# A decoder layer on one core: sums of squared encodings and router logits with the small matrix as the stationary operand, four token chunks on four column groups of TensorE

## The chip, the core and the metric

The kernel runs on one core of a Trainium2 chip. The core has a matrix engine (TensorE, PE in the profile), a vector engine (VectorE, DVE), a scalar engine for functions such as exp (ScalarE, ACT), a general engine (GpSimd, POOL), and a queue that issues most of the transfers (SyncE, SP). TensorE reads its operands from the on-chip memory SBUF and writes to the accumulator memory PSUM. A matrix product on it has two parts: a weight load puts the *stationary* operand into the array (PEld in the profile), and the matmul itself streams the *moving* operand through it. The engines run side by side and wait for each other through semaphores.

The metric is the time of one execution on the device in microseconds (us), median of nine runs: 1785.03 us for the kernel before, the lowest 1782.12, the highest 1790.69.

## What is computed

A decoder layer over 16 sequences of 256 tokens with 256 features (4096 tokens): a first attention, a cross attention, and a mixture of four experts, each followed by a residual sum and a layer norm. The two parts that matter here are the scores of the first attention and the router of the experts. The rest is cut.

```python
# first attention, 16 heads, 8 complex components a head
qp, kp = prep(Q), prep(K)                 # tanh of one product, then a second product
qc = qp[..., :nq] + 1j * qp[..., nq:]     # kc from kp in the same way
q1 = einsum('bshn,nm->bshm', qc, Hc)      # k1 in the same way
qe = real(einsum('hcb,bshn->cshn', R, q1))   # ke in the same way
qq = sum(qe ** 2, -1)                     # one number for each token and head
kk = sum(ke ** 2, -1)
s = qq[:, :, None, :] * kk[:, None, :, :]
attn = softmax(s / s, axis=2)
out = einsum('bijh,bjhd->bihd', attn, V).reshape(B, S, D) @ wo + bo

# router of the four experts, two of which each token takes
logits = einsum('bsh,he->bse', x, router_w) + router_b + load_balancer
rw, sel = top_k(logits, 2)
rw = softmax(rw)
```

`s / s` is the ratio of a product with itself. The kernel forms it from `p * (1 / p)` for each of the two factors: a *ratio* for the query side and one for the key side.

## The kernel before

All data is float32. The tokens are handled in eight *pairs* of sequences: a pair q has 512 tokens, which are four *chunks* n of 128 tokens (`CPB = 4`, `P = 128`). In the records of the profile each float32 product is two passes of TensorE (two LDWEIGHTS and two MATMUL records); a transposition is one.

**The order is written out by hand.** PE, ACT and DVE run their instructions in the order in which the program makes them (`ORDERED`, line 27). The first attention walks through 128 steps, 16 for each pair, numbered t. A step issues on TensorE first the product of the hidden layer (`hidden`, tile `ph`, four products), then the jobs that a planner hands out, then the second product of the step before (`outer`, tile `pe`, four products). ScalarE applies tanh to `ph` twice in each step (tile `h`). The two PSUM tiles `ph` are both used in each step, so that the next step's `ph` waits until ScalarE has read them.

**The planner** (`Plan`, line 30) holds jobs with a first step, a due step and a cost in us, which is a constant of the program. Each step grants a credit (`RATE`, line 850: 2.5 up to step 64, then 2.25); `spend` takes jobs in the order of their due steps while the credit lasts, and a job that is due is taken in any case. So costs and rate decide in which step a job's instructions stand, on all three ordered engines. The cross attention has a second planner (`planB`): its steps are called quarters (`quarter`, line 1360), four to a unit of a sequence and four heads; two quarters at a time get a credit (line 1586: 2.45). In the steps before and after a middle stretch (`SINGLE = 228`) jobs are taken one at a time instead.

**What the change touches in the first attention.** After eight steps of one side (keys are side 0, queries side 1) the tile `sq` holds squared encodings, 128 partitions by 512 tokens. For pairs 0 to 3 there is one such tile with eight partitions a head, for pairs 4 to 7 there are two (`sqs`). `norms` (line 966) sums the squares of each head: for each chunk n, the chunk of `sq` (128 by 128) is the stationary operand and a matrix of ones and zeros (`b16`, or `selc` where there are two tiles; 128 by 16) is the moving one. The result has tokens on partitions: 128 by 4 by 16. VectorE takes the reciprocal (`rc`) and multiplies (`ra`). On the query side the job `queries` (line 981) then turns the four chunks of `ra` by four transpositions into rows of heads (16 by 512, tile `ptr`), VectorE copies them to SBUF (`rqT`), and SP writes them to a buffer in DRAM (`rqd`). From there `spread` (line 1001) reads rows back, each repeated over all 128 partitions (`rqb`), four steps before `scores` (line 1009) multiplies them on VectorE with the key ratios of `ra` (tile `z`); `exps` takes the exponential on ScalarE and `weigh` (line 1033) multiplies with the values on TensorE (tile `po`, eight products with a 32-column stationary operand, four heads on four column groups).

**What it touches in the cross attention.** When the residual and norm of a pair are done, `turn_tokens` (line 1497) transposes its tokens to features on partitions (`xTr`, or `x` for the last two pairs), and the job `logits` (line 1511) multiplies: for each chunk n and each half c of the features the chunk (128 by 128) is stationary, the router's weights (128 by 4) move. VectorE adds the bias from PSUM (tile `lg`), and `routing` (line 380) goes on with small steps on VectorE, GpSimd and ScalarE, one in each of the next five steps. Six steps after `logits` the job `places` (line 1524) sums up positions on TensorE, and `listing` (line 431) scatters the tokens to the experts' lists in DRAM by indirect transfers on POOL's queue. After the last pair of a group (pair 6 for the first group, pair 7 for the second) the lengths of the lists are known, and the experts begin: `begin` (line 650) loads the first rows of a list (`xe`) and transposes them on TensorE.

Three stages follow each other: the first attention to about 560 us (its end overlaps the beginning of the next), the cross attention to about 1245 us, then the experts.

Of the kernel before, what the change touches and what calls it, by code (L numbers as in the profile page):

```python
# [22 lines left out]
CPB = TB // P  # L23
# [80 lines left out]
def decoder_kernel(ctx: ExitStack, tc: tile.TileContext, a: dict, out: bass.AP):  # L104
    nc = tc.nc
    PE, DVE, ACT, POOL, SP = nc.tensor, nc.vector, nc.scalar, nc.gpsimd, nc.sync
# [8 lines left out]
    ident = const.tile([P, P], F32, tag="ident", name="ident")  # L115
# [35 lines left out]
    def mm(out_, lhsT, rhs, start=True, stop=True):  # L151
        PE.matmul(out=out_, lhsT=lhsT, rhs=rhs, start=start, stop=stop)  # L152
# [189 lines left out]
    moe, puts = {}, ([], [])  # L342
# [7 lines left out]
    def moe_setup(wb, xw, xb, tri):  # L350
        moe["pool"] = wb

        def tl(name, shape, dt=F32):
            moe[name] = wb.tile(shape, dt, tag=name, name=name)
            return moe[name]

        moe["rw"], moe["rb"], moe["tri"] = xw[:, :, D:], xb[:, D:], tri
        before = tl("before", [P, P])
        POOL.memset(before, 1.0)
        POOL.affine_select(before, before, [[1, P]], ALU.is_gt, 0.0, base=0, channel_multiplier=-1)  # L360
        POOL.memset(tl("ones", [P, P]), 1.0)
        base = tl("base", [P, 2, 4])
        for g in range(2):
            for e in range(4):
                POOL.memset(base[:, g, e:e + 1], float(e * SIZES[g]))
        tl("place", [P, NCH, 2], I32)
        tl("weight", [P, NCH, 2])
        tl("count", [P, 2, 5], I32)
        tl("length", [P, 5])
# [463 lines left out]
    tl = tails.enter_context(tc.tile_pool(name="tl", bufs=1))  # L833
    dr = tails.enter_context(tc.tile_pool(name="drA", bufs=2, space=bass.MemoryType.DRAM))
# [9 lines left out]
    def first_attention():  # L844

        plan = Plan(
            turn_x=.55, project=1.85, values=1.85, norms=1.5, rotate=1.9, queries=.5, weigh=.9, finish1=.55, finish2=.55,
            finish3=1.9, fold=.8,
        )
        RATE = (2.5, 2.25)  # L850
        wk = mat(hd, "L0_attn_wk", D)
        w1p = hd.tile([P, 2, D], F32, tag="w1p", name="w1p")
        w2T = wH.tile([16, D], F32, tag="w2T", name="w2T")
# [24 lines left out]
        xTs, qTs, sums16, ratios, rqTs, rqbs, zs, ovs, os_, ots, encs, pes = ({} for _ in range(12))  # L878

        def bank(name):  # L880
            return banks[0].tile([P, 512], F32, tag="sm", name=name)
# [84 lines left out]
        def norms(q, side, sqs):  # L966


            p16 = bank("p16")[:, :CPB * H].rearrange("p (n h) -> p n h", h=H)
            for n in range(CPB):  # L970
                for i, sq in enumerate(sqs):
                    s = b16 if len(sqs) == 1 else selc[:, i, :]
                    mm(p16[:, n, :], sq[:, n * P:(n + 1) * P], s, i == 0, i == len(sqs) - 1)
            rc = tl.tile([P, CPB, H], F32, tag="rc", name=f"rc{q}{side}", bufs=2)
            DVE.reciprocal(rc, p16)
            ra = ratios[q, side] = tl.tile([P, CPB, H], F32, tag=f"ra{side}", name=f"ra{q}{side}", bufs=2)
            DVE.tensor_tensor(ra, p16, rc, ALU.mult)
            if side == 1:
                plan.job(plan.now + 1, plan.now + 1, queries, q)

        def queries(q):

            pw = bank("ptr")
            for n in range(CPB):
                PE.transpose(pw[:H, n * P:(n + 1) * P], ratios[q, 1][:, n, :], ident)
            rqT = tl.tile([H, 512], F32, tag="rqT", name="rqT", bufs=1)
            DVE.tensor_copy(rqT, pw[:H, :])
            rqTs[q] = dr.tile([H, 512], F32, tag="rqd", name="rqd")
            SP.dma_start(out=rqTs[q], in_=rqT)
            per = 1 if q < NPAIR - 1 else 2  # L990
            t0 = 16 * q + 25 if per == 1 else plan.now + 5
            for u in range(8):
                t = t0 + 2 * u // per
                plan.at(max(t - 4, plan.now + 1), spread, q, u)
                for gp in range(2):
                    plan.at(t + gp // per, scores, q, u, gp)
                    plan.at(t + gp // per + 1, exps, q, u, gp)
                tw = t + 1 // per + 2
                plan.job(tw, tw + 2, weigh, q, u)
# [9 lines left out]
        def scores(q, u, gp):  # L1009

            b, k = divmod(u, 4)
            z = zs[u, gp] = cm.tile([P, 2, 2, S], F32, tag="z", name="z", bufs=6)
            if q == NPAIR - 1 and gp == 1:
                return
            h0 = 4 * k + 2 * gp
            rk = ratios[q, 0][:, 2 * b:2 * b + 2, h0:h0 + 2].rearrange("p j h -> p h j")
            DVE.tensor_tensor(z, bc(rqbs[u][:, 2 * gp:2 * gp + 2], 2, 2), bc(rk, 3, S), ALU.mult)  # L1017

        def exps(q, u, gp):

            b, k = divmod(u, 4)
            z = zs[u, gp]
            if q < NPAIR - 1 or gp == 0:
                ACT.activation(z, z, AF.Exp)  # L1024
                return
            for g in range(2):
                for jc in range(2):
                    h = 4 * k + 2 + g
                    ACT.activation(
                        z[:, g, jc], rqbs[u][:, 2 + g], AF.Exp, scale=ratios[q, 0][:, 2 * b + jc, h:h + 1]  # L1030
                    )

        def weigh(q, u):
# [59 lines left out]
            DVE.tensor_scalar(w1p[:, par, :], w1p[:, 1, :], mpar[:, par:par + 1], None, ALU.mult)  # L1093
        project(0, 0, 0)

        b16 = tl.tile([P, H], F32, tag="b16", name="b16")
        POOL.memset(b16, 1.0)
        POOL.affine_select(b16, b16, [[-8, H]], ALU.is_ge, 0.0, base=0, channel_multiplier=1)
        POOL.affine_select(b16, b16, [[8, H]], ALU.is_ge, 0.0, base=7, channel_multiplier=-1)
        rep = wH.tile([H, 2, 8, 16], F32, tag="rep", name="rep")  # L1100
        POOL.memset(rep, 0.0)
        for cc in range(2):
# [8 lines left out]
            )  # L1111

        b8 = wH.tile([P, 8], F32, tag="b8", name="b8")
        selc = tl.tile([P, 2, H], F32, tag="selc", name="selc")
        POOL.memset(selc, 0.0)

        def halves():

            DVE.tensor_copy(b8, b16.rearrange("p (h t) -> p h t", t=2)[:, :, 0])
            for cc in range(2):  # L1120
                DVE.tensor_copy(selc[:, cc, 8 * cc:8 * cc + 8], b8)


        b2c = hd.tile([P, 1], F32, tag="b2c", name="b2c")
# [56 lines left out]
        for q in range(NPAIR):  # L1181
# [99 lines left out]
    def cross_attention(wb, r1, ps1):  # L1281
# [7 lines left out]
        for mp in mpads:  # L1289
# [4 lines left out]

        plan = Plan(
            finish1=.55, turn_x=.55, turn_keys=.55, turn_tokens=.55, finish4=.55, project=1.05, values=1.9, finish5=1.9,
            logits=1.9, places=.6, weigh=1.85,
        )
        turned_keys = set()
        SINGLE = 32 * NPAIR - 28  # L1300
# [1 line left out]
        def apart():  # L1302
            return 1 if plan.now >= SINGLE else 2
# [5 lines left out]
        def bank(name):  # L1309
            return banks[0].tile([P, 512], F32, tag="sm", name=name)  # L1310
# [183 lines left out]
        def slack(q):  # L1494
            return 3 if roomy(q) else 0
# [13 lines left out]
                plan.job(plan.now + apart(), plan.now + apart() + slack(q), logits, q)  # L1509

        def logits(q):
            pl = bank("pl")[:, :4 * CPB].rearrange("p (n e) -> p n e", e=4)
            for n in range(CPB):
                for c in range(2):
                    mm(pl[:, n, :], xTs[q, c][:, n * P:(n + 1) * P], moe["rw"][:, c, :], c == 0, c == 1)
            lg = tiny.tile([P, CPB, 4], F32, tag="lg", name="lg")
            DVE.tensor_tensor(lg, pl, bc(moe["rb"], 1, CPB), ALU.add)
            route = routing(q, lg)
            for k in range(5):
                plan.later(1 + k, next, route, None)  # L1520
            wait = (FREE - 9 - plan.now) % 16 if roomy(q) else 0
            plan.job(plan.now + 6 + wait, plan.now + 6 + wait + slack(q), places, q)
# [49 lines left out]
        def step(t):  # L1572

            if not 0 <= t < SINGLE:
                if 0 <= t // 4 < len(units) + LAG:
                    quarter(t // 4, t % 4)
                plan.run(t)
                if t < -3 or t % 4 > 0:
                    plan.take()
                else:  # L1580
                    plan.take(6)
            elif t % 2 == 0:
                for u in (t, t + 1):
                    plan.now = u
                    quarter(u // 4, u % 4)
                plan.grant(2.45)
                plan.run(t)
                plan.run(t + 1)
                plan.spend(most={"finish1": 2, "values": 1}, like={"logits": "values"})

        return plan, step

# [107 lines left out]
```

## Time and profile before

| | us |
|---|---|
| median of nine runs | 1785.03 |
| the profiled execution | 1783.59 |
| its span, first to last instruction | 1781.9 |
| TensorE matmul busy in the span | 1642.7 |
| ScalarE busy | 970.0 |
| VectorE busy | 919.7 |
| GpSimd busy | 539.0 |
| reciprocal in `norms` (L975), 16 of 0.557 | 8.9 |
| multiplication in `norms` (L977), 16 of 0.225 | 3.6 |
| copy in `queries` (L987), 8 of 0.678 | 5.4 |
| bias in `logits` (L1517), 8 of 0.172 | 1.4 |

How to read it: an instruction is given as line, engine, operation and tile (`out<-in`). Nearly all products have line 152, a helper, so they are told apart by tile and shape. `128*16` or `128*128` behind a PE operation are the rows and columns of the stationary operand that it uses, `32*128` is one with 32 rows (one of four row groups), `128*32` one with 32 columns (one of four column groups). A matmul's duration includes the way through the array, which overlaps with the next one; what a group of matmuls really takes is the distance from its start to the start of the next group, called its *pitch* below. The granted clock of TensorE is 1.00 in most of the span, 0.5 in single windows of 3.4 us, and the mean is 0.963.

### The profile page before, as it was taken

What the parts mean: (1) busy time and instruction counts of PE and PEld (TensorE: products, weight loads), DVE (VectorE), ACT (ScalarE), POOL (GpSimd) and SP (SyncE); (2) the same over time, 40 slices, a digit from 0 to 9 for tenths busy, and PEclk for the clock granted to TensorE, in tenths of its full rate; (3) what the DMA queues carried; (4) which work ended last, traced back from release to release, by engine and by line L of the source; (5) the groups of instructions that cost most, each with busy time, mean ns of one, the idle gap of its engine ahead of it and who ended that gap; (6) DMA issues with size and microseconds to landing.
All of it is one profiled execution on the core that took longest, in us unless ns stands there. A gap on an engine that the chain in (4) does not pass through costs nothing. (4 is left out here: it accounts for less than half of the span.)

```text
span 1781.9 us, 32316 instructions
## 1 busy us (share of the span) xinstructions
PE 1642.7 (92%) x12254; PEld 963.1 (54%) x12254; DVE 919.7 (52%) x1911; ACT 970.0 (54%) x1463; POOL 539.0 (30%) x1235
## 2 busy tenths in 40 slices
PE   7999999999999899999999999979999999899761
PEld 2344444444445556666666666644675758565551
DVE  2235565556556787777777777752223424122133
ACT  4457577778787766666666666534333122223127
POOL 5000332113213232334363553645330010131421
PEclk9999999999999999999999999987999999999976
DMA  9922111122122200000000000000352101221213
GB/s 254 295 90 71 58 62 61 60 70 87 60 72 73 96 15 14 2 3 26 26 21 20 26 9 20 32 31 32 99 183 73 48 1 49 85 80 46 66 49 124
DMA packets 117771, 115.34 MB, mean 65 GB/s; under 512 B 7776, under 2 KB 111408, under 8 KB 117584
## 3 DMA queue, kind: packets, MB, share of 16 engines
q1 hardware_dynamic: 108560, 93.08, 16.4%
q0 software_dynamic: 7824, 19.65, 3.7%
q8 instruction: 114, 1.87, 0.4%
q14 instruction: 73, 0.60, 0.1%
q10 hardware_dynamic: 1200, 0.15, 0.1%
HBM read 73.79 MB, written 38.54 MB: 63 GB/s over the span
## 5 line engine op out<-in xcount | busy, mean ns | idle before, releaser
L1392 DVE TENSOR_REDUCE mpad<-p 128x4 f32<-128x1024 f32 x256 | 303.2, 1218 | 122.5 <-PE p L152 108.2
L923 ACT ACTIVATE h<-ph,L_attn_b 128x1024 f32<-128x1024 f32 x256 | 271.3, 1111 | 158.8 <-PE ph L152 156.8
L1398 ACT ACTIVATE e<-p 128x512 f32<-128x512 f32 x512 | 269.6, 600 | 148.9 <-PE p L152 134.2
L152 PE MATMUL p<-qp,kT 32*128 32x256 f32 x2048 | 290.0, 400 | 3.5 <-issue 1.4
L152 PE MATMUL p<-kT,qp 32*128 32x256 f32 x2048 | 272.9, 395 | 7.5 <-DVE mpad L1392 6.5
L152 PEld LDWEIGHTS p<-qp,kT 32*128 32x128 f32 x2048 | 207.4, 188 | 22.5 <-PE p L152 6.7
L152 PEld LDWEIGHTS p<-kT,qp 32*128 32x128 f32 x2048 | 192.3, 185 | 49.6 <-DVE mpad L1392 22.9
L152 PE MATMUL ph<-qT,w1p 32*128 32x512 f32 x1024 | 160.3, 643 | 6.0 <-ACT h L923 3.9
L1017 DVE TENSOR_TENSOR z<-rqb,ra 128x1024 f32<-128x1024 f32 x120 | 151.3, 1266 | 3.7 <-DMA rqb<-rqd 2.4
L152 PE MATMUL pe<-h,w2p 128*32 128x512 f32 x1024 | 136.6, 604 | 0.0
L152 PE MATMUL pob<-e,vaug 128*32 128x512 f32 x1024 | 129.0, 623 | 0.2
L1024 ACT ACTIVATE z<-z 128x1024 f32<-128x1024 f32 x120 | 126.5, 1056 | 0.1
L152 PEld LDWEIGHTS ph<-qT,w1p 32*128 32x128 f32 x1024 | 45.5, 183 | 123.7 <-ACT h L923 67.8
L671 POOL DMA_INDIRECT ya<-xlist,place x44 | 42.2, 959 | 185.2 <-DVE h2T L519 52.4
L197 POOL TENSOR_SCALAR ln_ve<-ln_mv 128x2 f32<-128x2 f32 x32 | 7.2, 225 | 294.8 <-DVE ln_mv L195 294.1
L152 PE MATMUL pw<-xeT,L_ffn_sw_w 128*128 128x512 f32 (+1 forms) x256 | 85.0, 494 | 2.4 <-DVEq L713 2.4
L201 POOL TENSOR_SCALAR xs<-xs,ln_mv,rs_y 128x256 f32<-128x256 f32 x64 | 83.0, 1302 | 2.9
L152 PE MATMUL po<-z,vaug 128*32 128x256 f32 x1024 | 76.3, 397 | 6.0 <-ACT z L1024 4.3
L444 POOL DMA_INDIRECT xlist<-xs,place x64 | 64.1, 1001 | 50.5 <-DVE place L442 26.8
L152 PEld LDWEIGHTS pw<-xeT,L_ffn_sw_w 128*128 128x128 f32 x256 | 49.7, 195 | 36.2 <-issue 31.4
L571 ACT ACTIVATE hid<-pw 128x512 f32<-128x512 f32 (+1 forms) x32 | 15.7, 491 | 91.3 <-PE pw L152 61.5
L152 PE MATMUL pr<-L_ffn_ml_w,hid 128*128 128x256 f32 x288 | 63.1, 379 | 1.9 <-ACT hid L586 1.9
(366 smaller groups left out, 2603.1 us busy)
## 6 DMA issues: line engine op xcount, KB each, us to landing
rqb<-rqd SPq DMA_DIRECT2D x64, 512.0 KB
xlist<-zero SPq DMA_DIRECT2D x16, 1024.0 KB
xe<-xlist SPq DMA_DIRECT2D x20, 512.0 KB
xlist<-ye SPq DMA_DIRECT2D x14, 512.0 KB
xs<-in_x SPq DMA_DIRECT2D x8, 512.0 KB
cx<-in_ctx SPq DMA_DIRECT2D x8, 512.0 KB
qp<-st SPq DMA_DIRECT2D x256, 2.0 KB
out<-xs SPq DMA_DIRECT2D x8, 512.0 KB
```

Of the source, the lines that this page charges most:

```text
L152: PE.matmul(out=out_, lhsT=lhsT, rhs=rhs, start=start, stop=stop)
L197: POOL.tensor_scalar(ve, mv[:, :, 1], EPS, None, ALU.add)
L201: POOL.tensor_scalar(x, x, mv[:, i, 0:1], r[:, i:i + 1], ALU.subtract, ALU.mult)
L444: put = POOL.indirect_dma_start(xlist[g][:], bass.IndirectOffsetOnAxis(ap=place[:, n, k:k + 1], axis=0), xs[:, q * CPB + n, :], None)
L571: ACT.activation(h, pa, AF.Silu)
L671: POOL.indirect_dma_start(t[:, n, :], None, xlist[group(q)][:], bass.IndirectOffsetOnAxis(ap=moe["place"][:, q * CPB + n, k:k + 1], axis=0),)
L923: ACT.activation(h, phs[gp], AF.Tanh, bias=b1[:, fc:fc + 1])
L1017: DVE.tensor_tensor(z, bc(rqbs[u][:, 2 * gp:2 * gp + 2], 2, 2), bc(rk, 3, S), ALU.mult)
L1024: ACT.activation(z, z, AF.Exp)
L1392: DVE.tensor_reduce(mpads[j % 2][:, 2 * gp:2 * gp + 2, :, ic], p1, AX.X, ALU.max, negate=True)
L1398: ACT.activation(e[:, gi], p2[gi], AF.Exp)
```

## The change

In `norms` the small matrix becomes the stationary operand, and the squares move. `b16` and `selc` are stored twice side by side (32 columns: 16 heads, and the same 16 again), so that chunk n can be written to partitions 32n to 32n + 31 of one PSUM bank (`p32`, 128 by 128): the four chunks use four column groups. The ratios so come out as rows of heads. The reciprocal and the multiplication are done on 128 by 128. For the query side there is no job `queries` any more on TensorE: SP writes the four blocks of 16 rows to DRAM by four transfers, in the step of `norms`. For the key side a new job `keys` turns all four chunks with one transposition (128 by 128), and VectorE copies 128 by 64 of it to `ra`.

`logits` does the same with the router's weights, stored eight times side by side (32 columns, tile `rw`, made once by a copy on GpSimd). The result is a 128 by 128 tile in which 16 rows count; ScalarE copies it to SBUF (`lT`), and a new job `turn_logits`, two steps later (one in the last stretch), transposes it; VectorE adds the bias from there and `routing` starts.

The planner's costs are changed: `norms` 1.5 to 0.6, `queries` 0.5 is gone and `keys` 0.3 comes, `logits` 1.9 to 0.6, `turn_logits` 0.2 comes; the rates go from (2.5, 2.25) to (2.35, 2.1) and from 2.45 to 2.4. The rule that counted `logits` with `values` (at most one of both in two quarters) is gone.

```diff
-        moe["rw"], moe["rb"], moe["tri"] = xw[:, :, D:], xb[:, D:], tri
+        moe["rb"], moe["tri"] = xb[:, D:], tri
+        POOL.tensor_copy(tl("rw", [P, 2, 8, 4]), bc(xw[:, :, D:], 2, 8))
...
-            turn_x=.55, project=1.85, values=1.85, norms=1.5, rotate=1.9, queries=.5, weigh=.9, finish1=.55, finish2=.55,
+            turn_x=.55, project=1.85, values=1.85, norms=.6, rotate=1.9, keys=.3, weigh=.9, finish1=.55, finish2=.55,
...
-        RATE = (2.5, 2.25)
+        RATE = (2.35, 2.1)
...
         def norms(q, side, sqs):
-            p16 = bank("p16")[:, :CPB * H].rearrange("p (n h) -> p n h", h=H)
+            p32 = bank("p32")[:, :P]
+            for i, sq in enumerate(sqs):
+                s = b16 if len(sqs) == 1 else selc[:, i]
+                for n in range(CPB):
+                    mm(
+                        p32[32 * n:32 * n + 32, :], s.rearrange("p a h -> p (a h)"), sq[:, n * P:(n + 1) * P],
+                        i == 0, i == len(sqs) - 1,
+                    )
+            rc = tl.tile([P, P], F32, tag="rc", name=f"rc{q}{side}", bufs=2)
+            DVE.reciprocal(rc, p32)
+            DVE.tensor_tensor(rc, p32, rc, ALU.mult)
+            if side == 0:
+                plan.job(plan.now + 1, plan.now + 3, keys, q, rc)
+            else:
+                queries(q, rc)
+
+        def keys(q, rc):
+            pw = bank("ptr")
+            PE.transpose(pw[:, :P], rc, ident)
+            ra = ratios[q] = tl.tile([P, CPB, H], F32, tag="ra", name=f"ra{q}", bufs=2)
+            DVE.tensor_copy(ra, pw[:, :P].rearrange("p (n a h) -> p n a h", n=CPB, a=2)[:, :, 0])
+
+        def queries(q, rc):
+            rqTs[q] = dr.tile([H, 512], F32, tag="rqd", name="rqd")
             for n in range(CPB):
-                for i, sq in enumerate(sqs):
-                    s = b16 if len(sqs) == 1 else selc[:, i, :]
-                    mm(p16[:, n, :], sq[:, n * P:(n + 1) * P], s, i == 0, i == len(sqs) - 1)
...
-            if side == 1:
-                plan.job(plan.now + 1, plan.now + 1, queries, q)
-
-        def queries(q):
-            pw = bank("ptr")
-            for n in range(CPB):
-                PE.transpose(pw[:H, n * P:(n + 1) * P], ratios[q, 1][:, n, :], ident)
-            rqT = tl.tile([H, 512], F32, tag="rqT", name="rqT", bufs=1)
-            DVE.tensor_copy(rqT, pw[:H, :])
-            rqTs[q] = dr.tile([H, 512], F32, tag="rqd", name="rqd")
-            SP.dma_start(out=rqTs[q], in_=rqT)
+                SP.dma_start(out=rqTs[q][:, n * P:(n + 1) * P], in_=rc[32 * n:32 * n + H, :])
             per = 1 if q < NPAIR - 1 else 2
-            t0 = 16 * q + 25 if per == 1 else plan.now + 5
+            t0 = 16 * q + 25 if per == 1 else plan.now + 6
...
-            logits=1.9, places=.6, weigh=1.85,
+            logits=.6, turn_logits=.2, places=.6, weigh=1.85,
...
         def logits(q):
-            pl = bank("pl")[:, :4 * CPB].rearrange("p (n e) -> p n e", e=4)
-            for n in range(CPB):
-                for c in range(2):
-                    mm(pl[:, n, :], xTs[q, c][:, n * P:(n + 1) * P], moe["rw"][:, c, :], c == 0, c == 1)
+            pl = bank("pl")[:, :P]
+            for c in range(2):
+                for n in range(CPB):
+                    mm(
+                        pl[32 * n:32 * n + 32, :], moe["rw"][:, c].rearrange("p a e -> p (a e)"),
+                        xTs[q, c][:, n * P:(n + 1) * P], c == 0, c == 1,
+                    )
+            lT = moe["pool"].tile([P, P], F32, tag="lT", name="lT")
+            ACT.copy(lT, pl)
+            plan.job(plan.now + apart(), plan.now + apart() + slack(q), turn_logits, q, lT)
+
+        def turn_logits(q, lT):
+            pt = bank("ptl")
+            PE.transpose(pt[:, :P], lT, ident)
+            pl = pt[:, :P].rearrange("p (n a e) -> p n a e", n=CPB, e=4)[:, :, 0]
             lg = tiny.tile([P, CPB, 4], F32, tag="lg", name="lg")
             DVE.tensor_tensor(lg, pl, bc(moe["rb"], 1, CPB), ALU.add)
...
-                plan.grant(2.45)
+                plan.grant(2.4)
                 plan.run(t)
                 plan.run(t + 1)
-                plan.spend(most={"finish1": 2, "values": 1}, like={"logits": "values"})
+                plan.spend(most={"finish1": 2, "values": 1})
```

More of the change, by code (lines that the diff above doesn't have):

```diff
@@ L966, in norms @@
         def norms(q, side, sqs):
-            p16 = bank("p16")[:, :CPB * H].rearrange("p (n h) -> p n h", h=H)
-            for n in range(CPB):
-                for i, sq in enumerate(sqs):
-                    s = b16 if len(sqs) == 1 else selc[:, i, :]
-                    mm(p16[:, n, :], sq[:, n * P:(n + 1) * P], s, i == 0, i == len(sqs) - 1)
-            rc = tl.tile([P, CPB, H], F32, tag="rc", name=f"rc{q}{side}", bufs=2)
-            DVE.reciprocal(rc, p16)
-            ra = ratios[q, side] = tl.tile([P, CPB, H], F32, tag=f"ra{side}", name=f"ra{q}{side}", bufs=2)
@@ L977, in norms @@
-            DVE.tensor_tensor(ra, p16, rc, ALU.mult)
-            if side == 1:
-                plan.job(plan.now + 1, plan.now + 1, queries, q)
-        def queries(q):
-            pw = bank("ptr")
-            for n in range(CPB):
-                PE.transpose(pw[:H, n * P:(n + 1) * P], ratios[q, 1][:, n, :], ident)
-            rqT = tl.tile([H, 512], F32, tag="rqT", name="rqT", bufs=1)
-            DVE.tensor_copy(rqT, pw[:H, :])
-            rqTs[q] = dr.tile([H, 512], F32, tag="rqd", name="rqd")
-            SP.dma_start(out=rqTs[q], in_=rqT)
+            p32 = bank("p32")[:, :P]
@@ L1015, in scores @@
             h0 = 4 * k + 2 * gp
-            rk = ratios[q, 0][:, 2 * b:2 * b + 2, h0:h0 + 2].rearrange("p j h -> p h j")
+            rk = ratios[q][:, 2 * b:2 * b + 2, h0:h0 + 2].rearrange("p j h -> p h j")
             DVE.tensor_tensor(z, bc(rqbs[u][:, 2 * gp:2 * gp + 2], 2, 2), bc(rk, 3, S), ALU.mult)
@@ L1029, in exps @@
                     ACT.activation(
-                        z[:, g, jc], rqbs[u][:, 2 + g], AF.Exp, scale=ratios[q, 0][:, 2 * b + jc, h:h + 1]
+                        z[:, g, jc], rqbs[u][:, 2 + g], AF.Exp, scale=ratios[q][:, 2 * b + jc, h:h + 1]
                     )
@@ L1094, in first_attention @@
         project(0, 0, 0)
-        b16 = tl.tile([P, H], F32, tag="b16", name="b16")
+        b16 = tl.tile([P, 2, H], F32, tag="b16", name="b16")
         POOL.memset(b16, 1.0)
-        POOL.affine_select(b16, b16, [[-8, H]], ALU.is_ge, 0.0, base=0, channel_multiplier=1)
-        POOL.affine_select(b16, b16, [[8, H]], ALU.is_ge, 0.0, base=7, channel_multiplier=-1)
+        POOL.affine_select(b16, b16, [[0, 2], [-8, H]], ALU.is_ge, 0.0, base=0, channel_multiplier=1)
+        POOL.affine_select(b16, b16, [[0, 2], [8, H]], ALU.is_ge, 0.0, base=7, channel_multiplier=-1)
         rep = wH.tile([H, 2, 8, 16], F32, tag="rep", name="rep")
@@ L1113, in first_attention @@
         b8 = wH.tile([P, 8], F32, tag="b8", name="b8")
-        selc = tl.tile([P, 2, H], F32, tag="selc", name="selc")
+        selc = tl.tile([P, 2, 2, H], F32, tag="selc", name="selc")
         POOL.memset(selc, 0.0)
         def halves():
-            DVE.tensor_copy(b8, b16.rearrange("p (h t) -> p h t", t=2)[:, :, 0])
+            DVE.tensor_copy(b8, b16[:, 0].rearrange("p (h t) -> p h t", t=2)[:, :, 0])
             for cc in range(2):
-                DVE.tensor_copy(selc[:, cc, 8 * cc:8 * cc + 8], b8)
+                DVE.tensor_copy(selc[:, cc, :, 8 * cc:8 * cc + 8], bc(b8, 1, 2))
         b2c = hd.tile([P, 1], F32, tag="b2c", name="b2c")
```

## The prediction

> **What bounds the kernel now.** I read three views: the page's busy shares, the busy times by stage, and PE's timeline with its waits. The chain that ended last covers only the last 115 us (from 1666 to the end), which the change does not touch, so it decides nothing here.
>
> ```profile
> 350.00:420.00 70.00, 66.45 (x522) 29.68 (x514) 40.97 (x77) 52.26 (x54) 11.75 (x35) 1.00 0.22 73
> 420.00:490.00 70.00, 70.00 (x553) 30.41 (x546) 42.01 (x63) 55.82 (x57) 20.19 (x36) 1.00 0.21 65
> 560.00:620.00 60.00, 52.62 (x488) 29.61 (x484) 42.97 (x65) 46.12 (x81) 16.58 (x25) 0.97 0.30 98
> 900.00:1000.00 100.00, 99.45 (x1096) 66.50 (x1095) 73.06 (x143) 65.15 (x125) 55.10 (x140) 1.00 0.07 24
> 1200.00:1300.00 100.00, 93.45 (x454) 59.41 (x453) 25.14 (x75) 38.30 (x61) 41.23 (x111) 0.86 0.18 59
> ```
>
> Each line is a stretch: its length, then busy us of PE, weight load, DVE, ACT and POOL, the granted clock and the DMA share. In both attentions PE is busy 95 to 100%, with ACT at 65 to 80% and DVE at 58 to 76%. Where one ends and the other begins (560 to 620) and after 1200 it is not PE alone.
>
> Is a busy PE really the limit there? PE's timeline answers that (start, duration, group, number of passes):
>
> ```profile
> 402.21 1.06 PE L152 MATMUL pe<-h,w2p 128*32 128x512 f32 x8
> 403.21 1.14 PE L152 MATMUL ph<-qT,w1p 32*128 32x512 f32 x8
> 404.28 1.96 PE L152 MATMUL p<-selc,sq 128*128 128x16 f32 x16
> 406.17 1.07 PE L152 MATMUL po<-z,vaug 128*32 128x256 f32 x16
> 407.06 1.04 PE L152 MATMUL pe<-h,w2p 128*32 128x512 f32 x8
> ```
>
> Each group starts as soon as the one before lets it: pitches of 1.00 (`pe`), 1.07 (`ph`), 1.89 (the sums), 0.89 (`po`). I gave every group such a pitch and added them up step by step: for steps 17 to 127 this gives 463.6 us where the timeline has 479.7 (79.26 to 558.96), and most single steps agree within 0.1. The other 16.1 us are waits and half-clock windows, of which PE's waits name VectorE first:
>
> ```profile
> PE pex L1252 <- DVE scr L1250: 7.1, 7, 1.8
> PE pb L152 <- DVE rowsof L307: 2.4, 3, 1.4
> ```
>
> So PE work that is taken out of the first attention shortens it nearly one for one.
>
> **What a new group costs.** The trace has no matmul with 32 stationary columns and 128 moving. Its neighbours are `po` (same stationary shape, 256 moving, 0.89/16 = 55.6 ns a pass) and the load of 32 columns:
>
> ```profile
> L152 PEld LDWEIGHTS po<-z,vaug 128*32 128x32 f32 x1024 | 28.3, 111 | 50.1 <-issue 20.5 <-ACT z L1024 7.1 <-ACT z L1029 4.6
> ```
>
> 1024 loads keep the loader busy 28.3 us: 27.6 ns each, although one lasts 111, because four column groups overlap. A pass of half `po`'s length cannot take longer than `po`'s, and not less than its load: 27.6 to 55.6 ns. I take 45, nearer to `po`, because the last passes of a group must drain with nothing behind them. So 8 passes (pairs 0 to 3) take 0.36 us and 16 passes 0.72.
>
> [...]
>
> **Part by part, first attention (PE).**
> - `norms`, pairs 0 to 3: before 0.95 (0.91 to 0.99 in the timeline), after 0.36; eight times: -4.7.
> - `norms`, pairs 4 to 7: before 1.89, after 0.72. Seven of them lie in the steps: -8.2.
> - `queries`, four transpositions, 306.57 to 307.02, so 0.45; in their place `keys`, one. Single transpositions (`pex`, 381.05 to the next group at 381.28) take 0.23; I take 0.2 to 0.25. Seven against eight in the steps: -1.5.
>
> ```profile
> 306.57 0.61 PE L985 MATMUL ptr<-ident,ra 128*16 128x128 f32 x4
> 307.02 1.04 PE L1055 MATMUL pn<-ident,ovT 128*128 128x128 f32 x8
> ```
>
> Sum -14.4. The instruction order of the changed kernel holds the same jobs in the 128 steps otherwise; the lower rate only shifts some by a step or two, so nothing is pushed behind the last step.
>
> What takes some of it back is ScalarE. A step needs two tanh (1.111 each) and one exp (1.055), with a square (0.687) every fourth: 3.45 us. Steps in which PE needs less than 3.45 are more frequent now. If ScalarE could never catch up in a longer step, the sum of max(PE, 3.45) would lose 7.3 us before and 12.1 after. The real trace lost some 2.3 (steps 101, 104, 111, 117, 120 and 125, each 0.3 to 0.5 over its sum), about a third. So a third of the difference: +1.5; the bounds are 0 and +4.8.
>
> VectorE: a reciprocal of 128x64 takes 0.557 and one of 128x16 0.234, so 6.7 ns an element and 0.99 for 128 elements. The multiplication goes from 0.225 to some 0.29, the copy for `ra` costs some 0.22, and 0.678 (L987) falls away: per pair 2 x 0.50 + 0.22 - 0.68 = +0.54, 4.3 us in all. It lies under VectorE's free 40%. If that cover is gone, the copies out of PSUM queued behind it come late and PE pays up to those 4.3. `keys` waits for 1.3 us of VectorE, but 3 to 5 us of other PE groups stand between it and `norms` in the order.
>
> SP: four writes in place of one, 0.32 each, so 1 us a pair more, with the wait for VectorE as before. Behind them stand the reads of `rqb`, issued steps ahead; VectorE waited for those only twice, 2.4 us in all. POOL copies the router's weights once. Nothing on the path.
>
> **At the seam** (560 to 620) the last `norms` (-1.17) and the last `queries` with its wait (0.43 and 0.95, from 568.25 to 569.63) leave PE: -2.6. But ScalarE and VectorE are busy 46 and 43 of those 60 us with exps and `z`, which does not change. I take half, -1.3.
>
> **Cross attention (PE).** `logits`, 16 passes, goes from 764.42 to 766.23:
>
> ```profile
> 764.42 1.95 PE L152 MATMUL pl<-xw,xTr 128*128 128x4 f32 x16
> 766.23 0.63 PE L1469 MATMUL pto<-ident,ob 128*128 128x128 f32 x4
> ```
>
> That is 1.81; after 0.72, plus 0.25 for the transposition: -0.84 each, six pairs in the PE-bound part: -5.0. ScalarE gets a copy of 128 by 128: by 0.36 for 256 and 0.587 for 512 columns some 0.25, under its free third.
>
> For pair 6 it goes the other way. Its `places` starts the chain that fills the first group's lists, and PE then stands still until the list can be read:
>
> ```profile
> 1227.51 3.36 PE L152 MATMUL pob<-e,vaug 128*32 128x512 f32 x16
> 1230.80 0.38 PE L152 MATMUL pl<-accs,ones 128*128 128x4 f32 x2
> ...
> 1248.66 1.97 PE L518 MATMUL pt<-ident,xe 128*128 128x128 f32 x8 [4.12 <-DMA xe<-xlist]
> ```
>
> From 1230.80 to 1248.66 run the sums, eight scatters on POOL one after the other, and the load. In the new order `places` comes two quarters later, behind 16 more passes of `p` (1231.98 to 1233.80: 1.82). So -1.09 (logits) + 0.25 + 1.82 = +1.0. For pair 7 the transposition stands right behind `logits`, so PE waits for the copy: 0.25 + 0.3 + some 0.2 of signalling against -1.09: -0.3.
>
> **Sum:** -14.4 + 1.5 - 1.3 - 5.0 + 1.0 - 0.3 = -18.5 us. From the span of 1781.9 this gives 1763.4. The profiled run was 1783.59, the median of the nine 1785.03, 3.1 above the span: 1766 to 1767, and I say 1766. The experts' stage is left as it is.
>
> **Rivals.**
> - *ScalarE takes PE's place.* For it: 55.8 of 70 us busy, and new steps with hardly any job (120 has none). Against: it idled 159 us before `h`, nearly all of it for PE. With the full +4.8 in place of 1.5, nothing at the seam, and half of the cross attention's gain lost: 1766 + 3.3 + 1.3 + 2.5 = about 1773. Chance 0.16.
> - *The four column groups do not overlap at this length*, so the change does not do what it says. For it: a load lasts 111 ns alone, so a lone pass could cost as much as today's 118 (1.89/16). Against: the 27.6 of the same loads. Then only `queries` is gained, -1.5 and at the seam -0.7, while six transpositions cost +1.5, pair 6 +2.1, pair 7 +0.5: +1.9, 1787. Chance 0.07, and that is "the same".
> - *Slower: VectorE's lateness.* Place: steps 45 to 90, where PE runs folding jobs that wait for VectorE at once (`pex`, `rowsof`), 16.1 us of waits with the half-clock windows around them (`po` there took 1.70 instead of 0.89). Reciprocals of 1 us in front of such copies, and a new distribution of the jobs, can make each wait 1 to 3 us longer. It decides once those waits pass 16 + 18.5 = 35 us; at 38 the time is 1789. For it: nine such waits exist, and all move. Against: VectorE is 40% free and their number stays. Chance 0.11.
>
> **Numbers.** My forecast gets 0.66. A measurement of this kernel tells about 0.2% (3.6 us) from no change, so faster is under 1781.5: 0.66 + 0.16 = 0.82; same 0.07; slower 0.11. Range: at 27.6 ns a pass 320 passes gain 5.6 us more and shorter waits some 5: 1755. At 55.6 ns they lose 3.4, ScalarE takes 3.3 more, waits some 6: 1779.
>
> **What would show it.** `norms` of pairs 4 to 7 with a pitch of 0.5 to 0.9; the first attention's steps (from the first `ph` to the last) 10 to 17 us shorter; `logits` with a pitch of 0.5 to 0.9; `xe` ready about 1 us later after pair 6's `logits`; the experts as long as before. I am wrong if the new groups keep a pitch above 1.2, or if PE's waits for VectorE or ScalarE between 200 and 380 us grow by more than 10.

## The result, and the profile after

The changed kernel takes 1797.64 us (median of 10 runs, 1788.57 to 1802.06) where the kernel before, in the same rounds, takes 1785.07 (31 runs): ratio 1.0062, 95% interval 1.0048 to 1.0077. By the ratio it is some 11 us slower, not 19 faster. The profiled execution took 1790.21 us, its span 1788.5; it is one of the faster ones, so its trace shows less of the loss (6.6 us between the spans) than the medians do.

In the first attention, what the prediction looked at came out as forecast or better; in the cross attention it did not. First the busy times by stage of the changed kernel (columns as before: length, then PE, weight load, DVE, ACT, POOL, clock, DMA share, GB/s):

```profile
350.00:420.00 70.00, 67.81 (x549) 28.68 (x553) 42.92 (x76) 55.23 (x57) 16.64 (x37) 1.00 0.26 84
420.00:490.00 70.00, 69.76 (x529) 28.55 (x525) 41.29 (x65) 54.83 (x56) 20.06 (x48) 1.00 0.21 68
900.00:1000.00 100.00, 94.34 (x1002) 60.18 (x1002) 67.56 (x131) 61.62 (x119) 46.34 (x120) 0.97 0.07 23
1200.00:1300.00 100.00, 86.48 (x489) 54.86 (x490) 29.14 (x80) 42.17 (x69) 40.73 (x111) 0.91 0.18 59
```

In the first attention PE still works nearly all the time. In the middle of the cross attention (900 to 1000) it has fallen from 99.45 to 94.34 of 100 us, and the granted clock from 1.00 to 0.97: together some 8 per cent less work (94.34 x 0.97 = 91.5) in the stage in which 5 us were to be gained. Around the start of the experts (1200 to 1300) PE works 86.48 us in place of 93.45, at a granted clock of 0.91 in place of 0.86. PE's timeline of the changed kernel shows the new groups and the start of the experts:

```profile
362.62 0.64 PE L152 MATMUL p<-sq,selc 128*32 128x128 f32 x16
363.09 1.05 PE L152 MATMUL po<-z,vaug 128*32 128x256 f32 x16
...
748.88 0.64 PE L152 MATMUL pl<-xTr,rw 128*32 128x128 f32 x16 [0.18 <-ACT e L1406]
749.46 0.65 PE L1477 MATMUL pto<-ident,ob 128*128 128x128 f32 x4
...
1254.68 1.97 PE L519 MATMUL pt<-ident,xe 128*128 128x128 f32 x8 [9.86 <-DMA xe<-xlist]
```

`norms` has a pitch of 0.47 us where the old one took 1.89, `logits` 0.58 where it took 1.81: both below the forecast's 0.72. This `logits` is the first of eight, however; in the next four the group behind it (`pto`) starts 1.94 to 2.00 us after the start of `logits`, as late as before (1.81 to 2.04), which the part on the prediction takes up. The first list's rows (`xe`) come at 1254.68 where they came at 1248.66.

Two lists of waits of the changed kernel, VectorE's from 640 to 1200 us and PE's from 570 to 1250 (us in total, times, longest), say where the middle went:

```profile
DVE larger L397 <- POOL gt L394: 14.1, 6, 3.0
```

```profile
PE p L152 <- DVE o L1454: 11.3, 5, 2.5
PE pto L1477 <- POOL ob L1468: 6.5, 6, 1.4
```

In the kernel before, the first of these waits is

```profile
DVE larger L396 <- POOL gt L393: 4.2, 5, 0.8
```

the second does not occur at all, and the third comes once, with 1.4 us. To place them, I took the start of each of the 64 `pob` groups of PE (one for each unit of the cross attention, eight units to a pair) from the timelines of both profiles and subtracted; what a unit takes is counted below from the start of the group before it to the start of its own. The changed kernel leads by 14.3 us at unit 0 and by 15.8 at unit 14. At the first boundary between pairs that counts (units 16 and 17) it loses 2.3, though no list is written there yet (`larger` waits 0.83 us, PE 1.19 for `o`); at each of the next four it loses some 6: units 24 and 25 take 14.41 and 11.29 us where they took 10.23 and 9.73, and 32/33, 40/41 and 48/49 likewise. At unit 49 it is 12.3 us late. From there to the last unit it gets 12 back (6 of them at units 61 and 62, where the kernel before runs some 10 us at half clock and the changed one does not), at `xe` it is 6.0 late, at the end 6.6.

One such boundary on three engines of the changed kernel, first VectorE's timeline, then GpSimd's, then PE's:

```profile
1002.03 0.17 DVE L443 TENSOR_SCALAR place<-rf 128x2 int32<-128x2 f32 x1
1002.11 0.22 DVE L391 TENSOR_TENSOR gt<-lg 128x64 f32<-128x64 f32 x1
1002.24 0.22 DVE L392 TENSOR_TENSOR eq<-lg 128x64 f32<-128x64 f32 x1
1005.50 0.22 DVE L397 TENSOR_REDUCE larger<-gt 128x16 f32<-128x64 f32 x1 [3.04 <-POOL gt L394]
...
1005.99 0.42 DVE L1454 TENSOR_TENSOR o<-pn,rdb 128x256 f32<-128x256 f32 x1
```

```profile
1002.48 0.98 POOL L445 DMA_INDIRECT xlist<-xs,place  x1 [4.42 <-DVE eq L392]
1003.76 0.96 POOL L445 DMA_INDIRECT xlist<-xs,place  x1 [0.30 <-issue]
1004.74 0.33 POOL L393 TENSOR_TENSOR eq<-eq,tri 128x64 f32<-128x64 f32 x1
1005.15 0.32 POOL L394 TENSOR_TENSOR gt<-gt,eq 128x64 f32<-128x64 f32 x1
```

```profile
1006.47 0.79 PE L152 MATMUL p<-qp,kT 32*128 32x256 f32 x1 [2.54 <-DVE o L1454]
```

`routing` of one pair compares its logits on VectorE (`gt`, `eq`), lets GpSimd make two products of them, and takes the sum (`larger`) back on VectorE. In the same two quarters `listing` of the pair before issues two scatters. GpSimd ran the products behind the scatters: `eq` was done on VectorE at 1002.46, and its product started at 1004.74, 2.3 us later. VectorE stands at `larger` for 3.04 us, and behind `larger` stands `o`, which frees a PSUM bank that PE's next `p` needs. PE waits 2.54 us. The windows of the same stretch show the rest:

```profile
998.00:1002.00 4.00, 4.00 (x44) 2.54 (x37) 3.16 (x6) 2.60 (x6) 0.05 (x1) 1.00 0.00 0
1002.00:1006.00 4.00, 1.94 (x19) 1.25 (x18) 0.90 (x7) 1.83 (x4) 2.78 (x5) 0.97 0.21 72
1006.00:1010.00 4.00, 3.53 (x18) 1.87 (x22) 3.60 (x6) 1.13 (x3) 2.70 (x10) 0.50 0.00 0
1010.00:1014.00 4.00, 4.00 (x32) 1.42 (x28) 0.87 (x5) 0.76 (x3) 1.30 (x6) 0.68 0.00 0
```

After the wait PE runs at half clock: 4 us at 0.50 and 4 us at 0.68 are 3.3 us of lost work. With the 2.54 that is 5.8 us a boundary. In the kernel before the same products ran between the scatters, not behind them, as its GpSimd timeline shows:

```profile
998.28 0.32 POOL L392 TENSOR_TENSOR eq<-eq,tri 128x64 f32<-128x64 f32 x1 [2.29 <-DVE eq L391]
998.67 0.32 POOL L393 TENSOR_TENSOR gt<-gt,eq 128x64 f32<-128x64 f32 x1
...
1002.97 1.08 POOL L444 DMA_INDIRECT xlist<-xs,place  x1 [1.23 <-DVE mx L417]
```

Why the place changed: `places` (and with it each scatter) is set to a fixed quarter in sixteen by `FREE`, whenever the logits come. `routing` starts one quarter after the logits are there, and they are there two quarters later, since the job `turn_logits` follows `logits` by `apart()`, which is 2.

### The profile page after: what moved, and what is told of

The parts are those of the page before. It is cut to its first block, busy times and chain, and to the rows that moved or that the text cites. A ratio compares the mean times of both kernels' runs of the same rounds, so it can differ in the third digit from the quotient of the medians.

```text
span 1788.5 us, 32346 instructions
## 1 busy us (share of the span) xinstructions
PE 1629.4 (91%) x12238; PEld 940.7 (53%) x12238; DVE 923.2 (52%) x1911; ACT 970.7 (54%) x1471; POOL 541.0 (30%) x1236
## 5 line engine op out<-in xcount | busy, mean ns | idle before, releaser
L152 PE MATMUL p<-qp,kT 32*128 32x256 f32 x2048 | 301.0, 400 | 16.6 <-DVE o L1454 11.3
L152 PE MATMUL p<-kT,qp 32*128 32x256 f32 x2048 | 284.0, 399 | 6.0 <-DVE mpad L1400 6.0
L152 PEld LDWEIGHTS p<-qp,kT 32*128 32x128 f32 x2048 | 212.1, 187 | 40.0 <-DVE o L1454 15.2
L152 PEld LDWEIGHTS p<-kT,qp 32*128 32x128 f32 x2048 | 196.2, 186 | 57.2 <-DVE mpad L1400 25.9
L152 PE MATMUL ph<-qT,w1p 32*128 32x512 f32 x1024 | 166.1, 641 | 6.0 <-ACT h L924 4.2
L152 PE MATMUL pob<-e,vaug 128*32 128x512 f32 x1024 | 132.6, 639 | 0.0
L1433 ACT COPY ovTb<-pob 128x512 f32<-128x512 f32 x64 | 37.5, 585 | 61.4 <-PE pob L152 61.4
```

The lines of the kernel that those rows point to most:

```text
L1433: ACT.copy(o, po)
```

## The experiments

The theory, T1: those two quarters put routing's round trip behind the scatters, and the stall at the boundaries follows. The rivals: the new steps themselves (copy, transposition, column groups) cost the time; or the planner's lower rate and the dropped rule do (T3). The chips of the experiments run the kernel before in 1748 to 1749 us. The expectations of the first four were written for 1785, so they are compared by ratio (95% interval in brackets) or by the difference from the kernel before in the same rounds.

**The two halves.** `norms_only` has the changed kernel's first attention and the old router with its rate and rule, `router_only` the reverse. The edits are those parts of the diff above; `router_only` also makes two small buffers of the first attention single.

> The first half of the change alone: the sums of squares of the first attention in the new form, the router's logits, the rate of the second plan and its rule on values as before. T1 (the loss sits in the moved steps of routing at the pair boundaries of cross attention): the gain of the first attention and the seam stays (14.3 us at the first pob group) and nothing is lost behind it, so about 1785 - 14 = 1771 (1768 to 1775). Rival (the new rows and transposed keys of the first attention shift later work or the clock): it would be as slow as the changed kernel, 1790 or more.

> The second half alone: logits in column groups with copy, transposition and two quarters' delay, the second plan's rate and rules of the changed kernel; the first attention's sums as before (two small buffers of it are made single for space). T1: the loss of the pair boundaries (+26 to +28) and of the lists of the experts (+6) stands without the gain of 14, less the 12 that the last pair gave back: 1785 + 20 = about 1805 (1798 to 1812). VectorE waits about 3 us at each of 5 boundaries for POOL's gt. Rival (the halves are slow only together, by the phase of the plan against the half-clock windows): within 5 us of 1785.

Measured: `norms_only` 1737.68, ratio 0.9935 [0.9918, 0.9953], that is -11.2 us; `router_only` 1770.97, ratio 1.0119 [1.0101, 1.0137], +22.1 us. The sum, +10.9, is what the whole change costs. Both are as T1 expected (by the ratio, -14 with 10 to 17 allowed, and +20). The loss is all in the router's half, and the halves do not disturb each other. `router_only` has VectorE's 14.1 us of waits at `larger` again.

**The rate and the rule.**

```diff
-                plan.grant(2.4)
+                plan.grant(2.45)
...
-                plan.spend(most={"finish1": 2, "values": 1})
+                plan.spend(most={"finish1": 2, "values": 1}, like={"logits": "values"})
```

> The changed kernel with the second plan's rate (2.45 in place of 2.4) and its rule that logits and values share a limit as before; routing's comparison still falls in the scatters' step. T3 (the lower rate and the dropped rule rearrange the other jobs and cost the time): back to 1770 to 1778. T1: the boundaries stay slow, 1790 to 1800.

Measured: 1758.85, ratio 1.0055 [1.0037, 1.0074]. The kernel stays as slow as the changed one: T3 is out, as far as the rate and the rule go; no run puts the planner's old cost of `logits` back.

**Routing one quarter later.**

```diff
-                plan.later(1 + k, next, route, None)
+                plan.later(1 + k + roomy(q), next, route, None)
```

> The changed kernel with the five steps of routing one quarter later for pairs 0 to 5, so that its comparison falls behind the two scatters of the list as it did before. T1: VectorE's waits for POOL's gt fall from 14 us to about 5, the units at pair boundaries lose no more, and the time falls by 20 to 28 us: 1770 to 1777 (the 6 us at the start of the experts stay). Rivals (ScalarE's copy, the transposition, or the new order of the other jobs cost the time): 1795 to 1800, the boundaries as long as now.

Measured: 1761.72, ratio 1.0065 [1.0046, 1.0084]: nothing gained, the expectation missed. But the wait has moved. VectorE's timeline of this kernel:

```profile
1016.54 0.17 DVE L443 TENSOR_SCALAR place<-rf 128x2 int32<-128x2 f32 x1
...
1016.82 0.17 DVE L418 RECIPROCAL mx<-mx 128x4 f32<-128x4 f32 x1
1020.67 0.19 DVE L427 TENSOR_REDUCE weight<-eq 128x8 f32<-128x32 f32 x1 [3.67 <-POOL eq L425]
```

`larger` no longer waits, but routing's next round trip (`mx`, `nth` to GpSimd, `weight` back) now shares its two quarters with the next chunk's scatters, and waits 3.67 us. T1 had to be put more exactly: quarters go out two at a time and scatters come every four, so there are two phases, and a shift by one quarter only moves the other trip into the scatters. A shift by two restores the old phase.

**Routing two quarters later, after and before the change.** `route_two` is the changed kernel, `before_route_two` the kernel before, each with `plan.later(1 + k + 2 * roomy(q), next, route, None)` and nothing else.

> The changed kernel with routing's five steps two quarters (one pair) later for pairs 0 to 5, which is where they stood against the lists' scatters before the change: comparison in the pair behind the third chunk's scatters, the nth choice behind the fourth's, the weight in the pair after. T1 in its second form (each round trip from VectorE to POOL and back that shares a pair with scatters holds VectorE 3 us, and one quarter later only the next round trip was caught): waits for POOL's gt about 4 us in all, none above 1 us for its eq, pair boundaries as before the change, and 20 us less than the changed kernel, so 7 to 13 below the kernel before (ratio 0.993 to 0.996). Rivals (ScalarE's copy, the transposition, the later order of jobs): as the changed kernel, ratio 1.005 to 1.007.

> The kernel before with nothing but routing's five steps two quarters later for pairs 0 to 5: no column groups, no copy, no transposition. T1: it loses what the router's half of the change lost at the pair boundaries, 17 to 26 us (ratio 1.010 to 1.015), with VectorE waiting 3 us for POOL's gt at five boundaries. Rivals (the column groups, the copy or the transposition are what costs): within 3 us of the kernel before.

Measured: `route_two` 1734.10, ratio 0.9921 [0.9906, 0.9936], -13.9 us, a little better than expected; `before_route_two` 1779.25, ratio 1.0171 [1.0158, 1.0184], +31 us. This is the pair that decides. The one line brings the changed kernel from +11 to -14, and does to the old kernel, without any of the change's products, copies or transpositions, more than the router's half of it did (+31 against +22, and above the 17 to 26 expected). Windows of `route_two` at the same boundary:

```profile
992.00:996.00 4.00, 4.00 (x50) 2.20 (x42) 3.14 (x6) 2.35 (x5) 2.89 (x6) 1.00 0.21 72
996.00:1000.00 4.00, 4.00 (x43) 3.28 (x42) 3.42 (x7) 2.48 (x6) 1.99 (x10) 1.00 0.02 4
1000.00:1004.00 4.00, 3.71 (x42) 2.62 (x44) 3.86 (x14) 1.56 (x3) 2.51 (x5) 1.00 0.11 36
```

and of `before_route_two`, whose PE waits 2.88 us here:

```profile
1018.00:1022.00 4.00, 1.43 (x12) 1.28 (x16) 1.80 (x8) 0.08 (x1) 3.41 (x13) 0.73 0.19 67
1022.00:1026.00 4.00, 4.00 (x28) 1.86 (x25) 2.64 (x5) 2.41 (x5) 1.56 (x4) 0.50 0.02 6
```

In the first PE is busy and the clock 1.00 throughout; in the second there are the hole and the half clock of the changed kernel.

**The round trip taken away, no step moved.** `gt_vector` is the changed kernel with the two products on VectorE:

```diff
-        POOL.tensor_tensor(eq, eq, bc(moe["tri"], 1, CPB), ALU.mult)
-        POOL.tensor_tensor(gt, gt, eq, ALU.add)
+        DVE.tensor_tensor(eq, eq, bc(moe["tri"], 1, CPB), ALU.mult)
+        DVE.tensor_tensor(gt, gt, eq, ALU.add)
```

> The changed kernel with every step where it stands, and the two products of routing's first step (eq by tri, gt plus eq) on VectorE in place of GpSimd: VectorE works some 0.7 us a pair more, but has no round trip to wait for. T1: larger no longer waits for POOL, the 14 and 11 us units at the boundaries shrink to 10 to 11 and 10, and the time comes to within 5 us of route_two: ratio 0.991 to 0.996 against the kernel before. Rival (the boundaries are long because too many of VectorE's jobs fall into one pair, whoever waits): VectorE's added work makes them longer still, ratio 1.007 or more.

Measured: 1740.21, ratio 0.9941 [0.9921, 0.9962], -8.7 us. VectorE's timeline at the boundary:

```profile
998.37 0.22 DVE L392 TENSOR_TENSOR eq<-lg 128x64 f32<-128x64 f32 x1
998.62 0.24 DVE L393 TENSOR_TENSOR eq<-eq,tri 128x64 f32<-128x64 f32 x1
998.89 0.22 DVE L394 TENSOR_TENSOR gt<-gt,eq 128x64 f32<-128x64 f32 x1
999.15 0.22 DVE L397 TENSOR_REDUCE larger<-gt 128x16 f32<-128x64 f32 x1
```

The wait is gone, with every step where the change put it, and some 20 of the 25 us between the changed kernel and `route_two` with it. The ratio is the expected one, if just over 5 us from `route_two`'s; the units came down only in part, to 12.6 and 10.0 us, not 10 to 11 and 10. PE still waits up to 1.0 us for `o` at each boundary, with a shorter half-clock window around it (998 to 1002 at a mean of 0.77, 1002 to 1006 at 0.80). The rival, too many VectorE jobs in one pair of quarters, may hold for that smaller part; no run separates it.

**The scatters moved instead.** `lists_two` has `FREE = 8` in place of 6.

> The changed kernel with the lists' places and scatters moved instead of routing (their phase in the sixteen quarters from 6 to 8): the scatters then all stand ahead of the finished rows, far from routing. T1: no wait of VectorE for POOL's gt above 1 us, and the boundaries' 26 us come back unless the scatters now stand in front of POOL's other helpers (ob, hv, the reciprocal root), in which case some 2 to 3 us a pair stay: ratio 0.993 to 1.000. Rivals: as the changed kernel, 1.005 to 1.007.

Measured: 1742.11, ratio 0.9970 [0.9960, 0.9981], -5.9 us. The waits at `larger` are 0.8 at most, as expected; at the new place PE waits for `o` five times up to 1.2 us (5.9 in all). Separation helps from either side, and the new phase has its own price.

**The experts' start.** In the changed kernel pair 6's `places` comes two quarters later. Its scatters on GpSimd:

```profile
1241.30 0.96 POOL L445 DMA_INDIRECT xlist<-xs,place  x1 [0.30 <-issue]
1243.33 0.96 POOL L445 DMA_INDIRECT xlist<-xs,place  x1 [1.06 <-DVE place L443]
```

The fifth of eight waits for the `place` of its chunk, which stands on VectorE behind a reciprocal (`rdb`) that itself waits 5.12 us for PE's `pn`. `route_two_tail` and `route_two_six` put `places` back by two quarters, the first for pairs 6 and 7, the second for pair 6 alone:

```diff
-            plan.job(plan.now + 6 + wait, plan.now + 6 + wait + slack(q), places, q)
+            d = 6 + wait if q != NPAIR - 2 else 4
+            plan.job(plan.now + d, plan.now + d + slack(q), places, q)
```

> As route_two, and for pairs 6 and 7 the places come two quarters earlier (four after the logits are turned in place of six). T1: beside the gain of route_two the first list of the experts is ready 1 to 6 us earlier: 10 to 20 us below the kernel before (ratio 0.989 to 0.994). Rival (the six us at the experts' start came from the order of VectorE's conversions, which this doesn't change): no better than route_two.

> As route_two, and pair 6's places alone two quarters earlier (pair 7's stay, whose move cost the first group's products some 5 us again in route_two_tail). T1 with the tail's term: the first list is ready about 4 us earlier than in route_two and the rest follows: 3 to 5 us under route_two, ratio 0.989 to 0.991 against the kernel before. Rival (the gain at the lists is given back at the next transfers whatever pair 7 does): as route_two, 0.992 to 0.994.

Measured: `route_two_tail` 1738.46, ratio 0.9938 [0.9923, 0.9953], no better than `route_two`: the first list is ready 4.3 us earlier, but the first group's fifth transposition of `xe` starts 1.6 us later than in `route_two` (59.4 against 53.4 us after the first). `route_two_six` 1729.38, ratio 0.9901 [0.9879, 0.9922]: -18.7 us, as expected. PE's wait for `xe`, first in `route_two`, then in `route_two_six`:

```profile
1226.73 1.97 PE L519 MATMUL pt<-ident,xe 128*128 128x128 f32 x8 [9.82 <-DMA xe<-xlist]
```

```profile
1221.32 1.97 PE L519 MATMUL pt<-ident,xe 128*128 128x128 f32 x8 [4.47 <-DMA xe<-xlist]
```

This version is the best of all that ran.

**Both kernels again**, for profiles on a chip of the experiments.

> The kernel before, profiled on this chip, as the base of the unit times of the other runs. Both theories: ratio 1.000; pair boundaries as in the first trace (10.2 and 9.7 us), and VectorE's waits for POOL's gt 4 us in all.

> The changed kernel, profiled on this chip. T1: the same stalls as in its first trace (five boundaries with 14 and 11 us, VectorE waiting 14 us in all for POOL's gt): ratio 1.005 to 1.008. If the loss were a matter of the first chip, the ratio is 0.99.

Measured: 1.0009 [0.9994, 1.0024] and 1.0074 [1.0048, 1.0101]. The lead over `before_again` (us, from the starts of `pob` groups, of the first `pt` on `xe`, and the spans; below zero is earlier):

| | unit 0 | unit 23 | unit 50 | first `xe` | span |
|---|---|---|---|---|---|
| `after_again` | -13.3 | -15.7 | +11.0 | +9.6 | +6.0 |
| `norms_only` | -11.2 | -12.3 | -12.6 | -12.9 | -10.8 |
| `router_only` | +2.4 | +1.4 | +25.4 | +23.9 | +24.7 |
| `before_route_two` | +2.3 | +0.1 | +26.2 | +28.2 | +31.8 |
| `gt_vector` | -8.7 | -11.4 | +0.4 | -4.6 | -6.8 |
| `route_two` | -10.2 | -13.8 | -10.8 | -12.0 | -10.0 |
| `route_two_six` | -10.7 | -14.3 | -11.3 | -17.4 | -17.8 |

Between units 23 and 50 the kernels of this table that let a round trip share its quarters with scatters lose 24 to 27 us, `gt_vector` 12, `route_two` 3, and the kernel with the old router gains a little. Up to unit 0 several have the same instructions and differ by up to 5 us: that is the scatter of single profiles, of which `norms_only`, `router_only` and `gt_vector` come from other chips than `before_again`.

## Why the prediction was wrong

The step that failed is the one on the cross attention: "-0.84 each, six pairs in the PE-bound part: -5.0." It failed twice.

First, `logits` was counted by its own passes and its copy, and what the two quarters of delay move was followed for pair 6's `places` alone. For pairs 1 to 4 the same two quarters move `routing`'s first round trip over GpSimd into the scatters (`larger` waits 3.0 us in each; in pair 5 it is 1.07). That term was not in the sum. It costs some 6 us a pair.

Second, the saving itself did not come in these four pairs, because PE is not the limit at that place. The group behind `logits` is `pto`, which transposes `ob`, a product of GpSimd. PE's and GpSimd's timelines of the kernel before, then PE's of the changed one:

```profile
991.09 1.95 PE L152 MATMUL pl<-xw,xTr 128*128 128x4 f32 x16
993.05 0.65 PE L1469 MATMUL pto<-ident,ob 128*128 128x128 f32 x4
```

```profile
991.93 1.06 POOL L1460 TENSOR_TENSOR ob<-ob,rs_y 128x512 f32<-128x512 f32 x1
```

```profile
989.08 0.65 PE L152 MATMUL pl<-xTr,rw 128*32 128x128 f32 x16
991.04 0.66 PE L1477 MATMUL pto<-ident,ob 128*128 128x128 f32 x4 [1.31 <-POOL ob L1468]
```

In the kernel before, `ob` was done at 992.99 and `pto` started at 993.05: nothing was to spare. In the changed kernel `logits` is over 1.3 us earlier, and PE waits those 1.3 us for `ob`; `pto` starts 6.7 us behind the unit's `pob` in both. All kernels with the short `logits` wait 6.5 to 9.7 us in all for `ob`, the kernel before 1.4 to 1.6. So even with the phase put back (`route_two`) the eight units from the start of group 24 to that of 32 take 75.97 us where `before_again` takes 74.84: 1.1 us more, and not 0.84 less. They hold the same jobs, in part in other units; that the planner's new costs moved some of them may have a share in it. What sets the time of `ob` was not tried.

Between units 14 and 49 the changed kernel lost 28 us net to the kernel before on one chip and 27 on the other.

- **First attention and seam:** the sum is right, though not all of its terms. Forecast -14.4 + 1.5 - 1.3 = -14.2; measured at unit 0 -14.3 and, on the other chip, -13.3. But from the first `ph` to the last it is 547.22 to 535.32, -11.9, where -12.9 was forecast, although the groups of 16 passes there were shorter than forecast by some 1.7 us in all; so some 2.7 us more were taken back than the 1.5 of the sum, no run says by what, and the seam gave 2.4 in place of 1.3. That the total agrees is partly luck.
- **The price of a pass:** for eight passes 45 ns was right: `norms` of pairs 0 to 3 has a pitch of 0.36 us, as forecast, in six of eight groups. For 16 it was too high: 0.47/16 = 29 ns in `norms`, 0.58/16 = 36 in `logits`. In the trace's records of these groups four starts lie 6 to 7 ns apart, and the next four follow 89 to 114 ns behind them.
- **Pair 6:** direction right, size wrong: +1.0 forecast; 5.7 us were lost between the last `pob` and `xe` on one chip, 4.8 on the other. Against the last `pob`, the first of the eight scatters came 3.7 us later and the last 5.6. The two quarters were counted as their 16 passes; the conversions that fall behind `rdb`, and GpSimd's `ob` and its square between the last scatters, were missed.
- **Pair 7:** no run shows the 0.2 us of signalling as a time of its own. In the changed kernel PE stands 0.39 us between `logits` and the transposition, of which the copy takes 0.27.
- **The rivals:** ScalarE did not take PE's place, and the column groups overlap (four starts within some 20 ns, 29 to 36 ns a pass in groups of 16). The slower rival named VectorE's lateness, but in the first attention, where PE's waits hardly moved (`pex` from 5.6 to 7.0, `pb` from 2.4 to 1.6 between 200 and 380 us). It was the right engine in the wrong stage; what made it late was GpSimd's queue, which the prediction dismissed with "POOL copies the router's weights once. Nothing on the path."
- **The sum without the fault:** with the phase and pair 6's `places` put back, the measured ratio is 0.9901; times 1785 that is 1767, where 1766 was forecast. This too is partly luck. By the profiles of `route_two_six` and `before_again`, 10.7 us are gained up to unit 0, 0.6 between there and unit 50 (where most of the 5.0 was forecast), and 5.5 from unit 50 to the last `pob`, 3.8 of these at the last three units, for which the sum had no gain.

What made the change lose is shown: `before_route_two` reproduces it without the change, `route_two` and `gt_vector` remove most of it in two independent ways. Argued only is the share of the half-clock windows in it (3.3 of 5.8 us at the boundary shown), since no run has the wait without the window.

## What to carry to other kernels

When a change delays one step of a hand-written order, follow everything that hangs on that step by "so many steps later", not only the step that feeds the critical path: list for each of these which engines it hops between, and what stands ahead of it on each engine in the new place. A round trip from one engine to another and back inside the same step was cheap here only while the second engine's queue was empty; 2.3 us of scatters there became 3.0 us on VectorE, 2.5 on PE and 5.8 in time. And before time saved on one engine is counted as gained, look at what its next group needs: where that comes from another engine and has nothing to spare, the saving turns into a wait. If one part is fixed to a grid and the other floats, test the shift by moving the floating part a whole period, and make the same move in the old kernel: it separates the order from the new instructions in two runs.

## What the runs showed of the hardware

- Sixteen float32 passes with a stationary operand of 32 columns and 128 moving columns, on four column groups, took 0.46 to 0.47 us before another group of 32-column operands, 29 ns a pass, and 0.55 to 0.58 before one of 128 columns, where PE had nothing to wait for; eight passes took 0.36 before one of 128 columns and, in one group, 0.24 before one of 32. A pass of `po`, with 256 moving columns, took 0.89/16 = 55.6 ns, and the old ones 1.89/16 = 118: four times the 29.
- An indirect transfer of 128 rows of 1 KB occupied GpSimd's queue for 0.96 to 1.13 us (64 scatters in each of the two kernels), and where the next one had nothing to wait for, it started 1.26 to 1.44 us after the start of the one before. The two that started at 1002.48 and 1003.76 kept the next product off GpSimd for 2.3 us.
- At the boundary shown PE stood idle for 2.54 us, from 1003.93 to 1006.47; the granted clock went to 0.50 at 1005.8 and was back at 1.00 at 1012.6, 6.8 us later. In `gt_vector`, where PE waits at most 1.0 us for `o`, the two windows of 4 us from 998 to 1006 have mean clocks of 0.77 and 0.80, by which the half clock lasted an estimated 3.4 us ((0.23 + 0.20) x 4 / 0.5). In the kernel before, such stretches last 3.4 us each from 200 to 850 us, and 3.4 to 10.2 us from 1175 to 1255. What exactly triggers them was not tried.
